# Cross-attention and mixture-of-experts block: the second group's two projections, weight chunk requests and probability copies in new places of a hand-written order

## The chip, the cores and the metric

The kernel runs on one core of one Trainium2 chip. A core has TensorE (PE) for matmuls, VectorE (DVE), ScalarE (ACT), GpSimd (POOL) and SyncE (SP); here SP issues almost all DMAs. The engines run side by side, each through its own queue in order, and wait for each other by semaphores. The metric is the device time of one execution in microseconds (us).

## The reference

One transformer block on x of shape 32 x 100 x 512 with a context of which, by the causal mask, only the first 100 positions count. The first part is cross-attention with 16 heads of 32, the second a feed-forward part: a shared one for every token, and 16 experts that each pick their 12 best tokens per batch element.

```python
# cut to what matters
def attn(Q, K, V, WQ, WK, WV, Wfc, bfc):
    q, k, v = (heads(a @ W.T) for a, W in ((Q, WQ), (K, WK), (V, WV)))
    scores = jnp.einsum('bhqd,bhkd->bhqk', q, k) / jnp.sqrt(32.0)
    p = jax.nn.softmax(jnp.where(causal, scores, -jnp.inf), axis=-1)
    return merge(jnp.einsum('bhqk,bhkd->bhqd', p, v)) @ Wfc.T + bfc

def ffn(h, gate_w, Wg, Wu, Wd, Ws_g, Ws_u, Ws_d):
    w, idx = jax.lax.top_k(softmax(h @ gate_w.T).transpose(0, 2, 1), cap)
    out = scatter_add(idx, (gelu(h[idx] @ Wg.T) * (h[idx] @ Wu.T)) @ Wd.T * w)
    return out + (gelu(h @ Ws_g.T) * (h @ Ws_u.T)) @ Ws_d.T

x = x + attn(layernorm(x), ctx, ctx, ...)
x = x + ffn(layernorm(x), ...)
```

## The kernel before

Everything is float32 in and out. Each large matmul is done in three terms: an operand is split into a high part (rounded to the matmul's type, by a ScalarE copy) and a low part (the difference, by VectorE or POOL), and high x high, high x low and low x high are summed in PSUM (`mm3`, whose matmuls all carry line 56). So every operand of such a matmul costs a copy on one engine and a subtraction on another before TensorE can use it.

**Attention.** The 3200 tokens are cut into 8 blocks of 400 (4 batch elements), and the heads into 4 groups of 4. One *unit* u is one head group of one block, so there are 32 units (NU = 32). Per unit: project q (`qproj`), compute the scores of 4 x 4 pairs (`scores`, tile sc, line 240), take the row maxima on VectorE (`sm_max`, line 251), subtract them on POOL (`sm_sub`, line 260), exponentiate on ScalarE (`sm_exp`, line 264), sum on VectorE (`sm_sum`, line 269), multiply by the reciprocal on POOL (`sm_mul`, line 275), transpose the probabilities on TensorE (`p_turn`, line 281, called through `turns`), copy them from PSUM on ScalarE (`p_keep`, line 286, called through `keeps`), multiply with v (`values`, line 296), split the result and store it to DRAM (`y_keep`, lines 101, 102, 306). The softmax works in two halves (index 0 and 1) of 800 columns. The loop is pipelined by hand: while unit u is projected, u-1 is in its softmax and u-2 in its values.

**Feed-forward.** The tokens are cut into 9 groups of 3, 2, 3, 3, 3, 3, 3, 3 and 2 tiles of 128. For each group an object `Prep` makes the input: load y (`load_y`, tiles yh and yl) and x (`load_x`), add the bias on POOL (`bias`, line 1023), project y with Wfc (`fc`: 12 matmuls of 512 columns in a PSUM tile), add (`add`, line 1032), layer norm (`stats`, `rsqrt`, `norm`, lines 1038 to 1053), store for the experts' gathers, transpose (`turn`, line 963 on TensorE), and router logits (`logits`, `tokens`). Then `job` runs 8 steps f over chunks of the shared weights: 24 gate and up matmuls (tile gu), then 9 (6 for a group of two tiles) down matmuls (tile dn) of the step before. A weight chunk is 768 KB: `chunk_load` asks for the next one in turn, at most two are held raw, and the request for another waits until one of them has been split (`chunk_cast` and `chunk_low` by thirds, or `chunk_split` whole).

**The hand-over** is `last_units`, in which the last units' steps and the first groups' preparation are written out one after the other. The engines PE, ACT, DVE and SP run in the order in which their instructions are written there (`manual_schedule`); POOL too inside attention. Group 0 is projected during the last three units. Of group 1 (two tiles), the first tile is projected at the end of `last_units`, and the second in step f = 2 of group 0's job, from the tables that `run` fills; `early` counts what is already done. Only two PSUM tiles named kv and two named ms serve all projections and transposes there: a tile is free again only once its reader is done.

Of the kernel before, what the change touches and what calls it, by code (L numbers as in the profile page):

```python
# [60 lines left out]
def attention(tc, K, F):  # L61
    nc = tc.nc
    with ExitStack() as ctx, ExitStack() as kvctx:
# [143 lines left out]
        def kload(u):  # L207
            sb, c = divmod(u, NC4)
            kt = ktp.tile([128, SB], F32, name="kt")
            nc.sync.dma_start(kt, K.kD[:, c, sb * SB:(sb + 1) * SB])  # L210
            cur["k", u] = kt
# [50 lines left out]
        def sm_exp(u, hb):  # L262
            pv = cur["p", u, hb][1]
            nc.scalar.activation(pv, pv, AF.Exp)  # L264
# [24 lines left out]
        def values(u):  # L289
            sb, c = divmod(u, NC4)  # L290
            ys = ps_ms.tile([128, NC4, 128], F32, name="ms")
            for b in range(4):
                pt, v = cur["pt", u, b], cur["v", sb, b]
                for h in range(4):
                    d0 = c * 128 + 32 * h
                    nc.tensor.matmul(ys[32 * h:32 * h + 32, b, 0:S], v[:, d0:d0 + 32],  # L296
                                     pt[:, h, :], start=True, stop=True)
            cur["y", u] = ys
# [86 lines left out]
        def turns(u, *bs):  # L385
            for b in bs:
                p_turn(u, b)

        def keeps(u, *bs):
            for b in bs:  # L390
                p_keep(u, b)
# [8 lines left out]
        def last_units(pr):  # L400

            gp, mt = nc.gpsimd, pr.pt

            def maxes(u):
                for hb in range(2):
                    sm_max(u, hb)
                    sm_sub(u, hb)

            u = NU - 3
            scores(u - 1)  # L410
            kload(u)
            for i in range(pr.nt):
                pr.load_x(i)
            y_keep(u - 3)
            kload(u + 1)
            vload(nsb - 1)
            F.chunk_load()
            maxes(u - 1)
            qkeep(u, qproj(u))
            turns(u - 2, 0, 1)  # L420
            keeps(u - 2, 0, 1)
            turns(u - 2, 2, 3)
            sm_exp(u - 1, 0)
            keeps(u - 2, 2, 3)
            sm_exp(u - 1, 1)
            for hb in range(2):
                sm_sum(u - 1, hb)
                sm_mul(u - 1, hb)
            pr.fc(0)
            values(u - 2)  # L430

            u = NU - 2
            scores(u - 1)
            pr.add(0)
            y_keep(u - 3)
            F.chunk_load()
            pr.bias(0)
            maxes(u - 1)
            pr.bias(1)
            pr.stats(0)  # L440
            pr.rsqrt(0)
            qkeep(u, qproj(u))
            turns(u - 2, 0, 1)
            sm_exp(u - 1, 0)
            keeps(u - 2, 0, 1)
            sm_exp(u - 1, 1)
            pr.fc(1)
            for hb in range(2):
                sm_sum(u - 1, hb)
                sm_mul(u - 1, hb)  # L450
            turns(u - 2, 2, 3)
            keeps(u - 2, 2, 3)
            F.chunk_cast(0, 0)
            pr.norm(0)
            pr.add(1)
            kload(u + 1)
            values(u - 2)

            u = NU - 1
            scores(u - 1)  # L460
            y_keep(u - 3)
            pr.store(0)
            pr.bias(2)
            pr.stats(1)
            pr.rsqrt(1)
            maxes(u - 1)
            pr.norm(1)
            qkeep(u, qproj(u))
            F.ask(1, lambda: ps_kv.tile([128, D], F32, name="kv"))
            F.preps[1].load_x(0)  # L470
            F.preps[1].load_x(1)
            turns(u - 2, 0, 1)
            sm_exp(u - 1, 0)
            keeps(u - 2, 0, 1)
            sm_exp(u - 1, 1)
            pr.fc(2)
            sm_sum(u - 1, 0)
            sm_mul(u - 1, 0)
            pr.store(1)
            turns(u - 2, 2, 3)  # L480
            keeps(u - 2, 2, 3)
            sm_sum(u - 1, 1)
            sm_mul(u - 1, 1)
            pr.pt = lambda: ps_kv.tile([128, D], F32, name="kv").rearrange("p (c t) -> p c t", c=NC4)
            pr.turn(0)
            pr.pt = mt
            values(u - 2)
            pr.add(2)
            pr.turn(1)
            pr.stats(2)  # L490
            F.chunk_cast(0, 1)
            pr.rsqrt(2)

            scores(u)
            y_keep(u - 2)
            F.chunk_low(0, 0, gp)
            F.chunk_low(0, 1, gp)
            maxes(u)
            turns(u - 1, 0, 1)
            keeps(u - 1, 0, 1)  # L500
            turns(u - 1, 2, 3)
            keeps(u - 1, 2, 3)
            values(u - 1)
            pr.norm(2)
            sm_exp(u, 0)
            sm_sum(u, 0)
            sm_mul(u, 0)
            pr.turn(2)
            F.preps[1].fc(0)
            sm_exp(u, 1)  # L510
            sm_sum(u, 1)
            sm_mul(u, 1)
            y_keep(u - 1)
            pr.store(2)
            F.chunk_cast(0, 2)
            scctx.close()
            F.open_gu()
            F.begin(pr.done())
            F.chunk_low(0, 2, gp)
            F.preps[1].bias(0)  # L520
            F.preps[1].add(0)
            for i in range(3):
                F.chunk_cast(1, i)
                F.chunk_low(1, i, gp)
            F.preps[1].bias(1)
            turns(u, 0, 1)
            keeps(u, 0, 1)
            pr.logits()
            turns(u, 2, 3)
            keeps(u, 2, 3)  # L530
            F.begun()
            values(u)
            pr.tokens()
            y_keep(u)
# [91 lines left out]
class FeedForward:  # L626
# [186 lines left out]
    def run(self):  # L813
# [3 lines left out]
        def at(d, f, *calls):  # L817
            d.setdefault(f, []).extend(calls)
# [5 lines left out]
        for g in range(ng):  # L824
            mid, post = {}, {}
            p = preps.get(g + 1)
            early = 1 if g == 0 else 0
            if early:
                p.pm, p.pt = self.prep(1).pm, self.prep(1).pt
            if g == 0:  # L830
# [2 lines left out]
            if g < ng - 1:  # L833
                own = g == ng - 3
                z = 2 if own else 0
                if not early:
                    at(post, 0, *[lambda p=p, i=i: p.load_x(i) for i in range(p.nt)])
                if own:
                    for i in range(q.nt):
                        at(mid, i, lambda i=i: q.fc(i))  # L840
                        at(post, i, lambda i=i: q.ln(i))
                        at(post, 1 + i, lambda i=i: q.store(i))
                        at(mid, 2 + i, lambda i=i: q.turn(i))
                    at(post, 3, q.keep)
                    at(mid, 4, q.logits)
                    at(post, 4, q.tokens)
                    at(post, 1, lambda p=p: p.load_y())
                at(post, 1, *[lambda p=p, i=i: p.bias(i) for i in range(2 * early, p.nt)])
                for i in range(p.nt):
                    f = z + 1 + i  # L850
                    if i >= early:
                        at(mid, f, lambda p=p, i=i: p.fc(i))
                    if own:
                        at(post, f, lambda p=p, i=i: p.ln(i))
                        at(post, min(f + 1, 7), lambda p=p, i=i: p.store(i))
                        at(mid, min(f + 2, 7), lambda p=p, i=i: p.turn(i))
                    else:
                        f = (2, 3, 3)[i]
                        at(post, f, lambda p=p, i=i: p.ln(i))
                        at(post, f + 1, lambda p=p, i=i: p.store(i))  # L860
                        if g == ng - 2:
                            at(mid, 4 + i, lambda p=p, i=i: p.turn(i))
                        else:
                            at(post, f + 2, lambda p=p, i=i: p.quarters(i))
                            at(post, f + 3, lambda p=p, i=i: p.turn(i))
                if g == ng - 2:
                    at(mid, 7, p.logits)
                    at(post, 7, p.tokens)
                elif not own:
                    at(post, 7, p.logits)  # L870
                if g == ng - 4:
                    at(post, 6, q.load_y)
                    at(post, 6, q.load_rows)
                    at(post, 7, q.bias)
                    preps[ng - 2] = self.prep(ng - 2)
                elif g + 2 < ng:
                    at(post, 7, lambda g=g: self.ask(g + 2))
# [450 lines left out]
```

## Time and profile before

| | us |
|---|---|
| median of three runs | 1685.66 (1684.33 to 1686.12) |
| profiled execution | 1681.56 |
| its span, first to last instruction | 1679.3 |
| TensorE busy in the span | 1658.3 |
| start, 0 to 41 us of the span: TensorE busy | 34.38 of 41.00 |
| attention, 41 to 322: TensorE busy | 278.59 of 281.00 |
| hand-over, 322 to 374: TensorE busy | 45.70 of 52.00 |
| feed-forward, 374 to the end: TensorE busy | 1299.60 of 1305.30 |

In the views that follow, a line of the order of time has the start in us, the duration, the engine, the line of the kernel, the operation, output <- inputs by the program's tile names, the shape and the number of instructions; a bracket holds the idle time before it and what ended that. A line of the waits has who waited for whom, the total in us, how often, and the longest. Matmul durations overlap one another, so that the start of the next instruction tells more than the end of one.

### The profile page before, as it was taken

To read this page: it belongs to the slowest core of one execution; us is meant where nothing else is said; L and a number is where in the kernel's file an instruction comes from. 1 tells how busy PE (TensorE), PEld (TensorE's weight loads), DVE (VectorE), ACT (ScalarE), POOL (GpSimd) and SP (SyncE) were. 2 spreads that over 40 slices of the span, in tenths; PEclk is the share of its full clock that TensorE was granted. 3 is DMA by queue.
4 is the path that set the end of the run, shared out by engine and by line. 5 is a ranking of instruction groups with operands and counts; after the bars stand their busy time and mean duration, and the time that the engine had idled before them with its cause. 6 is when DMAs were issued, how large, how long until landed. Compare 5 with 4: busy or idle time off the path is not lost.

```text
span 1679.3 us, 28090 instructions
## 1 busy us (share of the span) xinstructions
PE 1658.3 (99%) x10879; PEld 1523.6 (91%) x10879; DVE 919.0 (55%) x2199; ACT 679.5 (40%) x1088; POOL 625.2 (37%) x542
## 2 busy tenths in 40 slices
PE   8999999989999999999999999999999999999999
PEld 7988888879889898989899999999999999999998
DVE  4878777665433434343555555555555555555542
ACT  4555555553111111112334444444444444444442
POOL 3778777670110011010243344333344333344011
PEclk9999999999999999999999999999999999999999
DMA  7555544555312223211455555455555455555452
GB/s 214 158 169 184 156 157 147 179 196 178 109 62 88 76 83 131 82 44 42 144 166 151 165 169 144 158 163 148 162 167 151 154 161 155 159 161 159 136 164 63
DMA packets 107125, 237.47 MB, mean 141 GB/s; under 512 B 14161, under 2 KB 58418, under 8 KB 106992
## 3 DMA queue, kind: packets, MB, share of 16 engines
q1 hardware_dynamic: 93632, 209.99, 38.4%
q0 software_dynamic: 12944, 25.22, 7.9%
q8 instruction: 85, 1.39, 0.4%
q10 hardware_dynamic: 416, 0.48, 0.1%
q14 instruction: 48, 0.39, 0.1%
HBM read 181.90 MB, written 53.73 MB: 140 GB/s over the span
## 4 chain that ended last, share of the span: by engine, by line
PE 93%; DMA 2%; DVE 1%; ACT 1%; POOL 1%; issue 1%; SPq 0%; ACTq 0%; POOLq 0%; DVEq 0%
PE gu L56 49%; PE dn L56 24%; PE kv L56 11%; PE m L56 3%; PE ms L281 2%; PE ms L296 1%; PE sc L240 1%; POOL p L260 1%; DMA v<-vD 1%; DVE p L251 1%; ACT pt L286 1%; PE ms L171 0%; DMA kD<-kk 0%; DMA x<-x 0%; DMA yh<-yD 0%
## 5 line engine op out<-in xcount | busy, mean ns | idle before, releaser
L56 PE MATMUL gu<-xh,whl 128*128 128x384 f32 (+1 forms) x3200 | 642.4, 332 | 0.0
L56 PEld LDWEIGHTS gu<-xh,whl 128*128 128x128 f32 x3200 | 556.7, 188 | 19.9 <-issue 1.7
L56 PE MATMUL dn<-whl,hh 128*128 128x512 f32 x1168 | 366.1, 394 | 0.0
L738 DVE TENSOR_TENSOR whl<-wraw,whl 128x1536 fp32r<-128x1536 f32 x142 | 249.8, 1759 | 203.2 <-ACT whl L737 181.6
L943 POOL DMA_INDIRECT gx<-xnD,iq x180 | 226.8, 1260 | 359.3 <-DVE big L974 299.8
L56 PE MATMUL gu<-xl,whl 128*128 128x384 f32 (+1 forms) x1600 | 336.7, 332 | 0.0
L56 PEld LDWEIGHTS gu<-xl,whl 128*128 128x128 f32 x1600 | 279.9, 188 | 0.0
L772 ACT CAST hh<-g 128x384 fp32r<-128x384 f32 (+1 forms) x200 | 100.9, 505 | 408.3 <-DVE g L769 384.2
L769 DVE TENSOR_TENSOR g<-g,gu 128x384 f32<-128x384 f32 (+1 forms) x200 | 108.4, 542 | 257.5 <-PE gu L56 252.9
L56 PEld LDWEIGHTS dn<-whl,hh 128*128 128x128 f32 x1168 | 215.5, 188 | 36.2 <-ACT hh L772 0.4
L737 ACT CAST whl<-wraw 128x1536 fp32r<-128x1536 f32 x142 | 210.0, 1479 | 61.8 <-PE dn L56 58.7
L56 PE MATMUL dn<-whl,hl 128*128 128x512 f32 x584 | 230.6, 395 | 0.0
L768 ACT ACTIVATE g<-gu 128x384 f32<-128x384 f32 (+1 forms) x200 | 96.3, 481 | 241.4 <-PE gu L56 240.7
L773 DVE TENSOR_TENSOR hl<-g,hh 128x384 fp32r<-128x384 f32 (+1 forms) x200 | 111.2, 556 | 114.2 <-ACT hh L772 113.7
L986 POOL DMA_INDIRECT out_dram<-x,isl x48 | 77.8, 1620 | 171.7 <-ACT x L985 161.9
L56 PEld LDWEIGHTS dn<-whl,hl 128*128 128x128 f32 x584 | 109.7, 188 | 25.3 <-DVE hl L773 0.2
L260 POOL TENSOR_TENSOR p<-p,mx 100x800 f32<-100x800 f32 x64 | 96.7, 1532 | 64.2 <-DVE mx L251 61.1
L275 POOL TENSOR_TENSOR p<-p,sm 100x800 f32<-100x800 f32 x64 | 101.2, 1582 | 4.7 <-DVE sm L270 3.9
L251 DVE CUSTOM_DVE_ANT_0 p<-sc,mask 100x100 f32<-100x100 f32 x512 | 95.4, 256 | 0.0
L1023 POOL TENSOR_TENSOR x<-x,bfc 128x512 f32<-128x512 f32 x23 | 30.6, 1347 | 155.1 <-DMA x<-x 119.5
L975 ACT CAST xh<-big 128x512 fp32r<-128x512 f32 x59 | 36.6, 621 | 101.2 <-DVE big L974 101.2
L269 DVE TENSOR_REDUCE sm<-p 100x8 f32<-100x800 f32 x64 | 63.1, 986 | 23.7 <-ACT p L264 23.7
(160 smaller groups left out, 1638.1 us busy)
## 6 DMA issues: line engine op xcount, KB each, us to landing
wraw<-wE SPq DMA_DIRECT2D x144, 768.0 KB
yD<-y SPq DMA_DIRECT2D x31, 400.0 KB
xt<-x SPq DMA_DIRECT2D x32, 200.0 KB
vD<-vt SPq DMA_DIRECT2D x25, 256.0 KB
kt<-kD SPq DMA_DIRECT2D x32, 200.0 KB
v<-vD SPq DMA_DIRECT2D x8, 800.0 KB
xnD<-xn SPq DMA_DIRECT2D x25, 256.0 KB
out_dram<-x SPq DMA_DIRECT2D x25, 256.0 KB
```

The costliest lines, as they stand in the source:

```text
L56: r = nc.tensor.matmul(out, t[0][a], t[1][b], start=(first and i == 0), stop=(last and i == n - 1))
L251: nc.vector.tensor_tensor_reduce(out=p[:, bb, h, :], in0=sc[:, h, cs], in1=mask, scale=ISCALE, scalar=NEG, op0=ALU.add, op1=ALU.max, accum ...
L260: nc.gpsimd.tensor_tensor(pv, pv, mx[:, :, None].to_broadcast([S, 8, S]), ALU.subtract)
L275: nc.gpsimd.tensor_tensor(pv, pv, sm[:, :, None].to_broadcast([S, 8, S]), ALU.mult)
L737: nc.scalar.copy(h, r)
L738: nc.vector.tensor_tensor(l, r, f32(h), ALU.subtract)
L768: nc.scalar.activation(g[:, 0:t], pg[:, 0:t], AF.Gelu)
L769: nc.vector.tensor_tensor(g[:, 0:t], g[:, 0:t], pu[:, 0:t], ALU.mult)
L772: nc.scalar.copy(hh[:, 0:t], g[:, 0:t])
L773: nc.vector.tensor_tensor(hl[:, 0:t], g[:, 0:t], f32(hh[:, 0:t]), ALU.subtract)
L943: nc.gpsimd.indirect_dma_start(out=g[:, k, :], out_offset=None, in_=self.K.xn.rearrange("t (a f) -> (t a) f", f=128), in_offset=bass.Indir ...
L986: ins = nc.gpsimd.indirect_dma_start(out=self.K.out, out_offset=bass.IndirectOffsetOnAxis(ap=r.isl[:, i:i + 1], axis=0), in_=o, in_offset= ...
```

## The change

Four things move; apart from that the instructions are the same.

- The first two requests for weight chunks (`chunk_load`) are written later: the first after group 0's first projection in the step u = NU-3, the second after the kt load at the end of the step u = NU-2.
- The casts of chunk 0 move back: the first from the step u = NU-2 to just ahead of the last scores, the second from there to between the two exponentials of the last unit. The low part of its second third moves from ahead of the last unit's maxima to after its second exponential.
- In the step u = NU-1 the first two probability copies are written ahead of the first exponential.
- Group 1's two projections stand inside the last unit: the first right after the last scores, the second after the transposes of unit 30. The values of unit 30 follow after the third tile's transpose. The second projection is no longer in step f = 2 of group 0's job, and both adds and both biases of group 1 are in `last_units`; bias comes after the split of chunk 1.

```diff
@@ step u = NU - 3
             vload(nsb - 1)
-            F.chunk_load()
             maxes(u - 1)
...
             pr.fc(0)
+            F.chunk_load()
             values(u - 2)
@@ step u = NU - 2
             y_keep(u - 3)
-            F.chunk_load()
             pr.bias(0)
...
-            F.chunk_cast(0, 0)
             pr.norm(0)
             pr.add(1)
             kload(u + 1)
+            F.chunk_load()
             values(u - 2)
@@ step u = NU - 1
             turns(u - 2, 0, 1)
+            keeps(u - 2, 0, 1)
             sm_exp(u - 1, 0)
-            keeps(u - 2, 0, 1)
             sm_exp(u - 1, 1)
...
             pr.stats(2)
-            F.chunk_cast(0, 1)
+            F.chunk_cast(0, 0)
             pr.rsqrt(2)
 
             scores(u)
             y_keep(u - 2)
             F.chunk_low(0, 0, gp)
-            F.chunk_low(0, 1, gp)
+            F.preps[1].fc(0)
             maxes(u)
             turns(u - 1, 0, 1)
             keeps(u - 1, 0, 1)
             turns(u - 1, 2, 3)
             keeps(u - 1, 2, 3)
-            values(u - 1)
+            F.preps[1].fc(1)
             pr.norm(2)
             sm_exp(u, 0)
+            F.chunk_cast(0, 1)
             sm_sum(u, 0)
             sm_mul(u, 0)
+            sm_exp(u, 1)
+            F.chunk_low(0, 1, gp)
             pr.turn(2)
-            F.preps[1].fc(0)
-            sm_exp(u, 1)
+            values(u - 1)
             sm_sum(u, 1)
             sm_mul(u, 1)
...
             F.chunk_low(0, 2, gp)
-            F.preps[1].bias(0)
             F.preps[1].add(0)
+            F.preps[1].add(1)
             for i in range(3):
                 F.chunk_cast(1, i)
                 F.chunk_low(1, i, gp)
+            F.preps[1].bias(0)
             F.preps[1].bias(1)
@@ FeedForward.run
-            early = 1 if g == 0 else 0
+            early = 2 if g == 0 else 0
...
-                at(post, 1, *[lambda p=p, i=i: p.bias(i) for i in range(2 * early, p.nt)])
+                at(post, 1, *[lambda p=p, i=i: p.bias(i) for i in range(early, p.nt)])
```

## The prediction

> **What bounds the kernel now.** I read the page first, then TensorE's own waits after the stage that the change edits, then the order of time of TensorE's instructions inside that stage, then those of the engines that release them.
>
> ```profile
> span 1679.3 us, 28090 instructions
> PE 1658.3 (99%) x10879; PEld 1523.6 (91%) x10879; DVE 919.0 (55%) x2199; ACT 679.5 (40%) x1088; POOL 625.2 (37%) x542
> ```
>
> TensorE is busy for 99% of the span. From 374 us on, where the feed-forward part runs alone, its waits come to two lines:
>
> ```profile
> PE m L963 <- DVE xl L965: 1.5, 1, 1.5
> PE m L1196 <- DVE x L1032: 0.2, 1, 0.2
> ```
>
> So a microsecond saved or lost before 374 should arrive at the end unchanged. Only two things can move the time: TensorE's work, which this change leaves equal in number, and TensorE's gaps in the hand-over between attention and feed-forward. These are the gaps (brackets: idle time, and what ended it):
>
> ```profile
> 348.33 1.09 PE L56 MATMUL kv<-wfh,yl 128*128 128x512 f32 x4
> 350.23 0.86 PE L281 MATMUL ms<-ident,p 100*100 100x100 f32 x8 [0.81 <-ACT pt L286]
> 350.93 0.67 PE L963 MATMUL kv<-ident,xn 128*128 128x128 f32 x4
> 351.80 0.89 PE L296 MATMUL ms<-pt,v 100*32 100x100 f32 x32 [0.20 <-ACT pt L286]
> 352.63 0.75 PE L963 MATMUL ms<-ident,xn 128*128 128x128 f32 x4
> 353.31 0.96 PE L240 MATMUL sc<-kt,q 32*100 32x100 f32 x32
> 354.87 0.52 PE L281 MATMUL ms<-ident,p 100*100 100x100 f32 x4 [0.60 <-DVE xl L965]
> 356.07 0.89 PE L281 MATMUL ms<-ident,p 100*100 100x100 f32 x8 [0.68 <-DVE y L102]
> 357.26 0.55 PE L281 MATMUL ms<-ident,p 100*100 100x100 f32 x4 [0.29 <-ACT pt L286]
> 357.74 1.09 PE L296 MATMUL ms<-pt,v 100*32 100x100 f32 x32
> 360.89 0.72 PE L963 MATMUL ms<-ident,xn 128*128 128x128 f32 x4 [2.06 <-DVE xn L1053]
> 361.37 1.17 PE L56 MATMUL kv<-wfh,yh 128*128 128x512 f32 x4
> ...
> 364.24 0.87 PE L56 MATMUL gu<-xh,whl 128*128 128x384 f32 x4
> ...
> 383.79 1.08 PE L56 MATMUL m<-wfh,yh 128*128 128x512 f32 x4
> ```
>
> The gaps sum to 0.81+0.20+0.60+0.68+0.29+2.06 = 4.64 us: the most that this change can win. Two instructions of other engines explain the largest:
>
> ```profile
> 358.84 1.91 DVE L1053 TENSOR_SCALAR xn<-x,mv,rs 128x512 f32<-128x512 f32 x1
> ...
> 358.93 3.20 POOL L260 TENSOR_TENSOR p<-p,mx 100x800 f32<-100x800 f32 x2
> ```
>
> The transpose at 360.89 needs the normalised third tile, which VectorE writes only after the 16 maxima of the last unit (356.01 to 358.9). Meanwhile TensorE has nothing else in its order.
>
> **The change part by part.**
>
> *Weight chunks asked for later.* I compared the orders on SP's queue. No SP instruction stands between the old and the new place of the first request, so it keeps its place behind the load of v. The second only changes places with one kt load (old issues: 335.31 and 335.87). kt is needed by the scores at 353.31 and the second chunk by casts behind 363; both DMAs had landed by 347 in the trace's landing records. Cost 0. The cover is at least 6 us for each.
>
> *First cast (chunk_cast(0,0)) taken out of the unit before.* ScalarE stood 1.23 us at 343.27 waiting for the chunk, and VectorE's y low part (L102, 344.31) then waited 0.27 us for ScalarE's y, queued behind that cast. Without it ScalarE's y starts at 342.7, when the values end; VectorE goes on at once, and the maxima, the first subtraction on POOL (347.28, which waited 0.35 us for them) and the second (ends 350.47) come 0.3 us earlier.
>
> *Probability copies ahead of exponentials (unit 31's step).* The first two copies run at 346.4 instead of 349.6, so the transposes of 350.23 start at 349.42: the 0.81 us gap closes. But copies 3 and 4 stand behind both exponentials, and the second exponential waits for POOL: 350.16, 0.87 us long, so copy 3 starts near 350.95 instead of 351.28. The values need copy 3's buffer and start 0.52 us after it begins (351.28 to 351.80), now at 351.47. The gap moves to the values; what remains is a gain of 0.33 us, all of it from the previous paragraph. The last scores start at 352.98.
>
> *Both projections (Prep.fc, 12 matmuls each) between softmax steps.* One costs 361.37 to 364.24 = 2.87 us of TensorE. New order with durations from the rows above (next start minus start):
> - scores 0.90, to 353.88;
> - fc(0) 2.87, to 356.75. It covers both the 0.60 and the 0.68 gap, whose releasers (VectorE at 354.7 and 356.0, now 0.3 earlier) are done by then;
> - four transposes of p: the first copy starts 0.61 us after the first transpose (354.87 to 355.48), and its buffer lets the third go 0.55 us later (the last copy of the pair to the next transpose, 356.71 to 357.26). So 0.61+0.55+0.35+0.39 = 1.90 us against 1.38 without waits, to 358.65;
> - fc(1) 2.87, to 361.52. It covers the 2.06 gap: maxima end at 358.6, norm between 359.1 and 360.8;
> - third tile's transpose 0.48, values 0.83, to 362.83.
>
> The gate matmuls also need ScalarE's xh (0.76 after the transpose starts, as 360.89 to 361.65, then 0.64) and, a quartet (0.70) later, VectorE's xl (0.61 after xh starts, then 0.84 as 354.03 to 354.87): 361.52+0.76+0.61+0.84 = 363.73, less 0.70 is 363.03. This ends last, by 0.2 us. The gate thus starts at an effective 363.03 instead of 364.24: 1.21 us.
>
> *The projection that leaves the feed-forward part* (383.79 to the next down matmul at 386.57): 2.78 us, off TensorE's path at a place without gaps.
>
> Sum: 1.21 + 2.78 = **3.99 us, taken as 4.0** (the 0.33 is inside the 1.21).
>
> *What each moved step meets.* fc(0) now needs yh and yl at 353.88 and 355.74 (two thirds through). Their issues (348.52, 349.45 on SP) wait only for the third projection, which does not move; by the landing records yh is complete at 352.35 and yl at 354.06. Slack 1.5 and 1.7 us. Were they later, all of TensorE's queue would stand behind fc(0): transposes, copies, values. POOL: one of the two low parts (1.28 us each) leaves the front of the last subtractions, which then start at 357.45 instead of 358.93, when the first maxima are done; the other goes between the multiplications, ends near 364.4, and is needed a quartet before the gate's end, about 366.5. The second multiplication ends near 366 and is needed by transposes near 369. The low parts of chunk 1 end at 371.0 (was 372.2). Bias after add: same instructions, ending at 373.5, needed at 387. VectorE's second add moves from 397 to 365, where it had 3.75 us of idle time. Chunk 4 lands 0.65 us before ScalarE turns to it, and its request moves with that chain; its matmuls come 5 us later. All 0.
>
> [...] VectorE's norm took 1.91 us at 358.84 and 1.81 at 341.63, both beside POOL's tensor work, but 0.58 at 348.51. [...]
>
> **The rivals.**
> - *Hand-offs eat part of it.* The transpose-copy-transpose ladder, or xh and xl ahead of the gate, cost 0.7 to 1.3 us more, or the 0.33 does not come. For it: the margin there is 0.2 us. Against: all links are measured ones. Gain 2.7 to 3.3 us: about 1682.7.
> - *All gaps close.* Gain 4.64 plus the 0.58 gap at 341 us: 1680.4. Against it: the ladder and the values' wait remain by my own working.
> - *The projection waits for its input (the slower side).* fc(0) stands first in TensorE's queue with yl still coming. Each microsecond beyond 355.74 delays everything: the gain is gone when yl lands at 359.7, 5.7 us later than now; 9.1 us late gives 1689. For it: this group's input loads were never waited for, so nothing has tested them. Against: before these two loads the DMA rate was near 0 (348 to 349.5 us), so there is nothing to queue behind, and the change adds no bytes there.
> - *The change doesn't do what it says:* true of the requests (above), not of the projections.
>
> **How the numbers follow.** The profiled execution took 1681.56 us (span 1679.3 and 2.3 around it); 4.0 less is 1677.6. The three runs shown have a median of 1685.66, 4.1 above the profiled one; the saving is in absolute time, so the forecast is 1681.7. The runs differ by 1.8 us; with 0.2% (3.4 us) as what can be told from no change, 4.0 is just outside. Chances: forecast 0.57, hand-offs 0.23, all gaps 0.05, slower 0.15 (late inputs and what I have not seen). The forecast's own range is 1680.6 to 1682.6, and some of it counts as no change; the hand-offs nearly all do. Faster 0.57, same 0.28, slower 0.15. Range: 1679.6 (all gaps, with 0.8 us of run-to-run difference) to 1687.0 (a little of the slower case).
>
> **What would show it.** In the changed profile: the 2.06 us gap before the third tile's transpose gone, the gate's first matmul near 363.0, no projection (m<-wfh,yh) in the third feed-forward step, that step's end 4 us earlier, TensorE's waits after 374 unchanged. The prediction is wrong if a kv<-wfh,yh projection carries a DMA wait, if the gate starts after 364, or if a weight wait turns up between 375 and 410.

## The result and the profile after

| | before | after |
|---|---|---|
| median, 11 runs each | 1684.31 us (1681.89 to 1686.12) | 1681.38 us (1677.50 to 1682.06) |
| profiled execution | 1681.56 us | 1681.51 us |
| its span | 1679.3 us | 1679.6 us |

The ratio is 0.9973, with a 95% interval of 0.9965 to 0.9981: a gain of 4.5 us (3.2 to 5.9); the medians differ by 2.9 us. The forecast was 1681.7 us, with a gain of 3.99 us worked out. The medians, the range and the sign agree with it. Yet the two *profiled* executions take the same time, and in the changed one the gate starts at 367.29 (1.40 us of that is a later start of the hand-over), which by the prediction's own signs (near 363.0; wrong if after 364) speaks against it. A gain that the medians show and the profiles don't has to be explained, and most of the experiments of the next section do that.

First, TensorE's waits of the changed kernel from 374 us to the end (who waited for whom, total us, times, longest):

```profile
PE m L965 <- DVE xl L967: 1.5, 1, 1.5
PE ms L296 <- ACT pt L286: 0.3, 1, 0.3
PE m L1198 <- DVE x L1034: 0.2, 1, 0.2
```

The feed-forward part waits as before: the 0.3 us are the last values (374.79), which stand at the border of this window. Next, the order of time of TensorE's instructions in the hand-over of the changed kernel:

```profile
350.74 0.85 PE L281 MATMUL ms<-ident,p 100*100 100x100 f32 x8
351.43 0.67 PE L965 MATMUL kv<-ident,xn 128*128 128x128 f32 x4
354.40 1.45 PE L296 MATMUL ms<-pt,v 100*32 100x100 f32 x32 [2.30 <-ACT pt L286]
355.78 1.13 PE L965 MATMUL ms<-ident,xn 128*128 128x128 f32 x4
356.84 1.48 PE L240 MATMUL sc<-kt,q 32*100 32x100 f32 x32
358.25 1.19 PE L56 MATMUL kv<-wfh,yh 128*128 128x512 f32 x4
...
361.13 0.85 PE L281 MATMUL ms<-ident,p 100*100 100x100 f32 x8
362.37 0.86 PE L281 MATMUL ms<-ident,p 100*100 100x100 f32 x8 [0.39 <-ACT pt L286]
363.01 1.17 PE L56 MATMUL kv<-wfh,yh 128*128 128x512 f32 x4
...
365.90 0.63 PE L965 MATMUL ms<-ident,xn 128*128 128x128 f32 x4
366.46 0.90 PE L296 MATMUL ms<-pt,v 100*32 100x100 f32 x32
367.29 0.96 PE L56 MATMUL gu<-xh,whl 128*128 128x384 f32 x4
...
386.23 0.86 PE L56 MATMUL gu<-xh,whl 128*128 128x384 f32 x4
386.92 0.62 PE L56 MATMUL dn<-whl,hh 128*128 128x512 f32 x2
```

From 358.25 on it is the picture that was forecast: neither projection waits for anything, the ladder of transposes has the one wait of 0.39 us, the third tile's transpose (365.90) has none where 2.06 us stood, and gate and up of the third step are followed at once by down (386.92), with no projection between. Ahead of it two things were not forecast: a wait of 2.30 us before the values (forecast: 0.72), and behind it values, transposes and scores that take 1.45, 1.13 and 1.48 us, against 0.89, 0.75 and 0.96 before.

What the values wait for, followed back through the order of time of the other engines of the changed kernel:

```profile
343.20 3.20 DVE L1055 TENSOR_SCALAR xn<-x,mv,rs 128x512 f32<-128x512 f32 x1
...
346.93 0.56 DVE L102 TENSOR_TENSOR y<-ms,y 128x400 fp32r<-128x400 f32 x1
...
343.12 3.01 POOL L275 TENSOR_TENSOR p<-p,sm 100x800 f32<-100x800 f32 x2
...
349.88 3.19 POOL L260 TENSOR_TENSOR p<-p,mx 100x800 f32<-100x800 f32 x2 [0.61 <-DVE mx L251]
...
351.44 0.87 ACT L264 ACTIVATE p<-p 100x800 f32<-100x800 f32 x1 [2.76 <-POOL p L260]
353.10 0.87 ACT L264 ACTIVATE p<-p 100x800 f32<-100x800 f32 x1 [0.79 <-POOL p L260]
353.87 0.87 ACT L286 COPY pt<-ms 100x400 f32<-100x400 f32 x2
```

The same pair of instructions in the profile before, VectorE's normalisation of the first tile (`norm(0)`) and GpSimd's two multiplications:

```profile
341.63 1.81 DVE L1053 TENSOR_SCALAR xn<-x,mv,rs 128x512 f32<-128x512 f32 x1
...
341.55 3.28 POOL L275 TENSOR_TENSOR p<-p,sm 100x800 f32<-100x800 f32 x2
```

In both profiles the normalisation (line 1055 in the changed kernel) starts 0.08 us behind the first multiplication. In the changed kernel it ends 0.27 us behind the second and takes 3.20 us, and each multiplication takes 1.53 us; before, it took 1.81 us and ended 0.37 us behind the first multiplication, and there the second took 1.80 us, so that the two took 3.28 us instead of 3.01. The starts don't tell which of the two outcomes it will be. Behind the normalisation queue the low part of y, the maxima, through them GpSimd's subtractions, and then the second exponential, behind which copies 3 and 4 stand in ScalarE's order.

The granted clock of TensorE in three consecutive stretches of the changed kernel (columns: stretch, its length, busy time of PE, PEld, DVE, ACT and POOL, granted clock, share and rate of the DMA engines):

```profile
351.16:354.57 3.41, 1.11 (x18) 0.92 (x19) 2.29 (x6) 2.34 (x4) 2.77 (x3) 1.00 0.98 301
354.57:357.98 3.41, 3.41 (x64) 2.79 (x60) 2.32 (x5) 1.69 (x5) 2.18 (x2) 0.50 0.67 230
357.98:361.39 3.41, 3.41 (x31) 2.73 (x24) 3.38 (x25) 0.46 (x2) 2.15 (x4) 1.00 0.29 104
```

For 3.41 us right behind the wait the clock is 0.50, and the three long steps lie in that stretch.

### The profile page after: what moved, and what is told of

Same layout as the page of the kernel before. It is cut to its first block, busy times and chain, and to the rows that moved or that the text cites. A ratio compares the mean times of both kernels' runs of the same rounds, so it can differ in the third digit from the quotient of the medians.

```text
span 1679.6 us, 28091 instructions
## 1 busy us (share of the span) xinstructions
PE 1660.7 (99%) x10879; PEld 1526.4 (91%) x10879; DVE 920.8 (55%) x2199; ACT 679.2 (40%) x1088; POOL 625.2 (37%) x542
## 3 DMA queue, kind: packets, MB, share of 16 engines
q8 instruction: 85, 1.39, 0.3%
## 4 chain that ended last, share of the span: by engine, by line
PE 93%; DVE 2%; ACT 1%; POOL 1%; DMA 1%; issue 1%; SPq 0%; ACTq 0%; POOLq 0%; DVEq 0%
PE gu L56 49%; PE dn L56 24%; PE kv L56 10%; PE m L56 3%; PE ms L281 2%; PE ms L296 2%; POOL p L260 1%; PE sc L240 1%; DVE p L251 1%; DMA kD<-kk 1%; ACT pt L286 1%; PE ms L171 0%; DVE y L102 0%; PE m L1109 0%; DMA raw<-wA 0%
```

## The experiments

In the table, all durations come from each kernel's profiled execution. Waits are those from unit 30's scores on. "Hand-over" runs from the start of unit 30's scores (342.58 in the profile before, 343.98 after) to the first gate matmul; that leaves out what comes earlier, which differs by up to 2.5 us between the profiles (the scores of the first unit alone start between 41.24 and 43.14 us). "Rest" is from there to the end of the span. The forecast's hand-over was 363.03 - 342.58 = 20.45 us. Each ratio is to the runs of the kernel before that were made in the same rounds; their medians lie between 1684.31 and 1684.74 us.

| kernel | median us (runs) | ratio to before (95%) | norm(0) us | waits over 0.7 us | half clock | hand-over | rest |
|---|---|---|---|---|---|---|---|
| before | 1684.31 (11) | 1 | 1.81 | 0.81, 2.06 | no | 21.66 | 1315.06 |
| e0, before again, two profiles | 1685.37, 1686.02 | | 3.21, 3.21 | 1.92, 2.07 in each | twice in each | 25.44, 25.34 | 1314.98, 1315.03 |
| after | 1681.38 (11) | 0.9973 (0.9965-0.9981) | 3.20 | 2.30 | once | 23.31 | 1312.31 |
| e1, after again | 1680.01 (7) | 0.9971 (0.9960-0.9982) | 3.21 | 2.30 | once | 23.42 | 1312.40 |
| e2, projections alone | 1679.01 (6) | 0.9968 (0.9955-0.9980) | 3.21 | 1.94 | no | 21.84 | 1312.20 |
| e3, all but them | 1682.63 (13) | 0.9992 (0.9983-1.0000) | 1.81 | 0.77, 0.83 | once | 21.57 | 1315.26 |
| e4, after, all copies first | 1677.98 (5) | 0.9961 (0.9948-0.9975) | 3.21 | none | no | 20.89 | 1312.36 |
| e5, after, norm(0) on ScalarE, late | 1683.40 (13) | 0.9995 (0.9986-1.0003) | 0.82 | 2.33 | no | 22.25 | 1314.02 |
| e7, e4 and e5 | 1680.84 (11) | 0.9977 (0.9968-0.9986) | 0.81 | 0.71 | no | 21.69 | 1314.10 |
| e8, after, norm(0) on ScalarE, early | 1679.71 (6) | 0.9965 (0.9953-0.9977) | 0.81 | 1.11 | no | 20.48 | 1314.08 |
| e9, before, norm(0) on ScalarE, early | 1686.98 (13) | 1.0012 (1.0004-1.0021) | 0.81 | 1.67, 2.08 | no | 22.46 | 1316.92 |
| e10, e4 and norm(0) as in e8 | 1678.79 (5) | 0.9958 (0.9944-0.9971) | 0.81 | none | no | 19.76 | 1314.13 |
| e11, after, wait filled | 1679.59 (5) | 0.9964 (0.9951-0.9978) | 3.20 | 0.79 | no | 21.71 | 1312.48 |

### Both kernels again, unaltered

> The changed kernel once more, unaltered. Its runs lie in two groups, near 1677.9 and near 1681.6. [...] Theory 2 (start-up): the groups differ in what happens before 45 us of the span, and the hand-over looks alike in both, with the 3.20 us norm and the gap in it.

The changed kernel again: 1680.01 us, ratio 0.9971 (0.9960 to 0.9982). Its profile repeats all of the first: norm(0) 3.21, wait 2.30, half clock (355.81 to 359.22), hand-over 23.42. So the wait is no accident of one execution. Whether a quick run has a norm(0) near 1.8 us and no half clock in the hand-over, or parts from the others by 45 us of the span, could not be put to the test, as the profile did not fall among the quick runs; and four of these seven runs lie between the two groups, which are less sharp than they looked. Taken together, the 18 runs of this kernel have a median of 1680.1.

> The kernel before once more, unaltered, for its trace alone: its median is 2.9 us above the execution that was profiled first. Theory 1 (hand-over): an execution near 1684 shows the norm of the first tile (L1053 near 342) at 3.2 us, or TensorE at half clock for 3.41 us between 350 and 364, or both, and the gate starts 2 to 3.5 us later than 21.66 us after the scores of 342 us. Theory 2 (start-up): all of the difference is there by 45 us of the span.

> As the look before, to see whether the outcome of the norm and of the clock changes from execution to execution of one kernel (then they are chance) or stays (then they belong to the kernel).

The kernel before, twice: 1685.37 and 1686.02 us. Both look different from the profile that the forecast was made on. TensorE's order of time in the first of the two (release in brackets), and the granted clock in the stretches behind those two waits:

```profile
351.54 0.86 PE L281 MATMUL ms<-ident,p 100*100 100x100 f32 x8 [1.92 <-ACT pt L286]
...
363.23 1.05 PE L963 MATMUL ms<-ident,xn 128*128 128x128 f32 x4 [2.07 <-DVE xn L1053]
```

```profile
353.17:356.58 3.41, 3.41 (x56) 2.79 (x60) 2.22 (x5) 1.59 (x4) 2.29 (x2) 0.50 0.69 240
...
363.41:366.82 3.41, 3.41 (x11) 2.83 (x11) 2.93 (x5) 2.80 (x6) 2.58 (x2) 0.50 0.00 0
```

norm(0) took 3.21 us in both, the 0.81 us wait of the first profile is 1.92 here, and behind each of the two waits the clock is halved for 3.41 us. The hand-over takes 25.4 us. The profile before, 4.1 us under the median of the three runs shown with it, was an execution in which norm(0) took 1.81 us and the clock stayed at 1.00 behind every wait of the hand-over. That explains most of the equal profiled times: they compare a lucky execution of one kernel (hand-over 21.66) with an unlucky one of the other (23.31). Taken apart, the changed kernel's span is 1.40 us longer up to unit 30's scores, 1.65 us longer in the hand-over and 2.75 us shorter in the rest, together 0.3 us longer. Unlucky against unlucky the hand-over gains 25.4 - 23.4 = 2.0 us, and the rest 2.7. How often each outcome comes was not counted: all four of these executions lie above the medians of their kernels.

### The two halves of the change

e2 is the kernel before with only the projections, their adds and biases, and the values of unit 30 moved (the second projection is left out of step f = 2 accordingly):

```diff
             F.chunk_low(0, 1, gp)
+            F.preps[1].fc(0)
             maxes(u)
...
-            values(u - 1)
+            F.preps[1].fc(1)
             pr.norm(2)
...
             pr.turn(2)
-            F.preps[1].fc(0)
+            values(u - 1)
...
             F.preps[1].add(0)
+            F.preps[1].add(1)
...
```

> The kernel before with the two projections of group 1 moved (and add and bias after them) and nothing else: chunk requests, casts and copies as before. If the gain is the projections' (my sum: 3.99 less the 0.3 that the cast and copies bring), the median is 3.5 to 4 us under before, within 1 us of the changed kernel. If the gain came from casts, copies or requests, it is within 1.5 us of before.

1679.01 us, ratio 0.9968: 5.4 us under the kernel before, more than the 3.5 to 4 expected. TensorE's order of time in e2:

```profile
351.20 0.86 PE L281 MATMUL ms<-ident,p 100*100 100x100 f32 x8 [1.94 <-ACT pt L286]
...
362.82 0.63 PE L965 MATMUL ms<-ident,xn 128*128 128x128 f32 x4
```

The 2.06 us wait is gone and with it, in this execution, any half clock, though norm(0) took 3.21 us here too and the wait ahead of the transposes stood at 1.94 us. Its hand-over of 21.84 us less the 1.19 us by which its values came later than in the profile before (10.41 against 9.22 us from the start of the scores) is 20.65: by this estimate, which takes the later start of the values as passed on in full, the projections alone gained 21.66 - 20.65 = 1.0 us there, and another 1315.06 - 1312.20 = 2.86 us in the rest.

e3 is the reverse, the changed kernel with the projections back in their old places (bias stays where the change put it):

```diff
             F.chunk_low(0, 0, gp)
-            F.preps[1].fc(0)
             maxes(u)
...
-            F.preps[1].fc(1)
+            values(u - 1)
             pr.norm(2)
...
             pr.turn(2)
-            values(u - 1)
+            F.preps[1].fc(0)
...
```

> The changed kernel with the projections put back where they were before (one after the third tile's transpose, one in step f = 2); requests, casts and copies as in the change. By my sum 0.3 us under before, not to be told from it: ratio 0.999 to 1.001. If requests, casts and copies carry the gain, ratio near 0.997.

1682.63 us, ratio 0.9992 (0.9983 to 1.0000): no change that can be told. So the whole of the gain that can be told from no change belongs to the projections, as the sum said. In e3's profile norm(0) took 1.81 us, as in the profile before, and so the copies' order can be read without that disturbance: the values start 8.81 us after the scores instead of 9.22, 0.41 us earlier (forecast 0.33), with 0.77 us of the wait left (forecast 0.72).

### Where the copies stand

e4 takes the changed kernel and puts copies 3 and 4 ahead of the second exponential as well:

```diff
             sm_exp(u - 1, 0)
-            sm_exp(u - 1, 1)
             pr.fc(2)
...
             turns(u - 2, 2, 3)
             keeps(u - 2, 2, 3)
+            sm_exp(u - 1, 1)
```

> The changed kernel with copies 3 and 4 of that step also written ahead of the second exponential. Theory 1: the values no longer wait for the exponential that POOL holds up, so the 2.30 us gap (and the half clock after it) goes and the group near 1681.6 moves down by 2 us or more; in the fast group the remaining 0.7 us gap goes as well: median 1677 to 1678.5, one group rather than two. Theory 2: two groups 3.6 us apart remain, and the median goes down by 0.7 at most.

1677.98 us, all five runs between 1677.38 and 1678.69: 2 us under the changed kernel's median in e1, and the ratio to the one before is 0.9961 (6.6 us; the intervals of the two ratios overlap). TensorE's order of time in e4:

```profile
351.62 0.89 PE L296 MATMUL ms<-pt,v 100*32 100x100 f32 x32 [0.64 <-ACT pt L286]
...
354.72 1.19 PE L56 MATMUL kv<-wfh,yh 128*128 128x512 f32 x4 [0.63 <-DVE xl L967]
```

norm(0) still took 3.21 us, yet the values wait 0.64 us instead of 2.30: once the copies no longer stand behind an exponential, its lateness reaches only work that isn't needed yet. The hand-over falls by 2.4 us (23.31 to 20.89); a wait of 0.63 us for a transposed tile's low part is new.

### Is norm(0) the cause?

e5 moves norm(0), and no other tile's, from VectorE to ScalarE, which computes rs * x + nm with nm = -mean * rs made on GpSimd:

```diff
-        nc.vector.tensor_scalar(xn, self.xb[i], mv[:, 0:1], rs, ALU.subtract, ALU.mult)
+        if (self.t0, i) == (0, 0):
+            nm = F.stp.tile([128, 1], F32, name="nm")
+            nc.gpsimd.tensor_scalar(nm, mv[:, 0:1], rs, -1.0, ALU.mult, ALU.mult)
+            nc.scalar.activation(xn, self.xb[i], AF.Identity, bias=nm, scale=rs)
+        else:
+            nc.vector.tensor_scalar(xn, self.xb[i], mv[:, 0:1], rs, ALU.subtract, ALU.mult)
```

> The changed kernel with the norm of group 0's first tile on ScalarE (with its bias made by one small POOL operation), so that VectorE no longer waits for POOL's multiplications there. Theory 1: maxima, subtractions and exponentials come 1.2 to 1.6 us earlier, the 2.30 us gap shrinks to 0.7, the half clock behind it goes: one group, 1677 to 1678. Theory 2: still two groups, near 1678 and 1681.5.

> Copies 3 and 4 ahead of the second exponential and the norm of the first tile on ScalarE together. If each removes its own wait, 0.5 to 1.5 us under the kernel with the copies alone (1677.98), that is 1676.5 to 1677.5; if the second one only removes what the first already covers, no difference from it.

1683.40 us, and 1680.84 with e4's copies: 2.0 to 3.4 and 2.9 us slower than without the edit, which none of the expectations had. The edit was badly placed. Orders of time of ScalarE and of GpSimd in e5:

```profile
345.60 0.82 ACT L1058 ACTIVATE xn<-x,nm,rs 128x512 f32<-128x512 f32 x1 [2.92 <-POOL nm L1057]
...
345.30 0.27 POOL L1057 TENSOR_SCALAR nm<-mv,rs 128x1 f32<-128x1 f32 x1
```

nm stood in GpSimd's queue behind both multiplications, so ScalarE waited 2.92 us, and its y, on which VectorE's chain hangs, stood behind it. So the values still waited 2.33 us, now for another reason. This profiled execution (1681.52 us) is 1.9 us under e5's median; what the slower ones contain was not seen. These two decide nothing on norm(0), but e5 tells something of the clock, below.

e8 makes nm right behind rs, ahead of the multiplications:

```diff
         nc.gpsimd.tensor_tensor(rs, rs, F.K.nhalf[:, 0:1], ALU.pow)
+        if (self.t0, i) == (0, 0):
+            nm = F.stp.tile([128, 1], F32, name="nm")
+            nc.gpsimd.tensor_scalar(nm, mv[:, 0:1], rs, -1.0, ALU.mult, ALU.mult)
...
```

> The changed kernel with the first tile's normalisation on ScalarE instead of VectorE, its bias (minus mean times rs) made on GpSimd right behind rs, so ahead of the two multiplications by 1/sum; in e5 the bias stood behind them and so ScalarE waited 2.92 us. Theory 1 (VectorE's 3.2 us normalisation at 342 to 343, held up by GpSimd's two multiplications of 100x800, delays maxima, subtractions and exponentials, and so the last copies): the wait of the values before the last scores falls from 2.30 to about 0.8 us, no half-clock stretch stands behind it, and the time is 1677.5 to 1679.0 in all runs, near e4. Rival (the normalisation is late for another reason, or something else sets the exponentials): the wait stays over 1.8 us and the time stays at 1680 to 1681.5.

ScalarE, VectorE and TensorE in e8, by their orders of time:

```profile
344.31 0.81 ACT L1060 ACTIVATE xn<-x,nm,rs 128x512 f32<-128x512 f32 x1
...
345.53 0.58 DVE L102 TENSOR_TENSOR y<-ms,y 128x400 fp32r<-128x400 f32 x1 [0.93 <-ACT y L101]
...
353.94 0.89 PE L296 MATMUL ms<-pt,v 100*32 100x100 f32 x32 [1.11 <-ACT pt L286]
...
365.32 0.97 PE L56 MATMUL gu<-xh,whl 128*128 128x384 f32 x4
```

VectorE's y starts 0.69 us after the scores, against 2.95 in the changed kernel; the wait of the values falls from 2.30 to 1.11 us, no clock is halved, and the hand-over takes 20.48 us, where 20.45 had been forecast. So norm(0) is the cause of 1.19 us of the wait of 2.30 us in the profile of the changed kernel; without these no clock was halved behind the wait. The time misses both expectations (1677.5 to 1679.0, or 1680 to 1681.5): the median, 1679.71 us, is lower by only 0.3 to 1.7 us than the two medians of the changed kernel, and the runs still spread from 1678.16 to 1681.21; the rest, from the gate on, is 1.77 us longer (last section), which hides part of the gain. The profiled execution is the slowest of the six; its scores start late, at 344.84.

> The kernel before with the same edit of the first tile's normalisation. Theory 1: the wait of the probability turns for GpSimd falls from 1.92 to 0.8 us or less, the wait of 2.06 us behind the last scores stays with its half-clock stretch; 1682.0 to 1683.5 us, ratio 0.9985 to 0.9995. Rival (before doesn't suffer from that normalisation): 1684.0 to 1685.0 and a ratio of 1.

The same edit in the kernel before gave 1686.98 us, slower by 0.12% (0.04 to 0.21%), where a gain or no change was expected. ScalarE's order of time in e9:

```profile
343.74 0.62 ACT L721 CAST whl<-wraw 128x512 fp32r<-128x512 f32 x1 [1.31 <-DMA wraw<-wE]
344.27 0.81 ACT L1058 ACTIVATE xn<-x,nm,rs 128x512 f32<-128x512 f32 x1
```

There the first cast of the weight chunk stands ahead of the normalisation, and waits 1.31 us for its DMA. VectorE's y comes 2.57 us after the scores, hardly better than 2.95. That is one part of why nothing was gained; the longer rest, here 1.9 us, is another. This profiled execution (1684.17 us) is 2.8 us under e9's median and shows no half clock; what the slower runs contain was not seen.

> The best version so far (e4, all four copies ahead of the second exponential) with the same edit. Theory 1: the copies no longer wait for the exponential, so the earlier exponentials can only help the turns of the last unit: 1677.3 to 1678.2, the same as e4 within 0.5 us. Rival (ScalarE's added 0.6 us stands in the way of its copies): 1678.5 or more.

1678.79 us, ratio 0.9958, not to be told from e4 (0.9961); the median lies in the range of the rival, but not for its reason. Its hand-over is the shortest of all, 19.76 us; the rest, 1.77 us longer than e4's, takes that back. The simple e4 is the better version.

### Is it the wait that halves the clock?

e11 leaves the wait of the values as it is and puts TensorE work nobody needs into it: the four transposes of the first tile are issued four times, into the same places.

```diff
-        for b in range(NC4):
+        for b in list(range(NC4)) * (4 if fill else 1):
             nc.tensor.transpose(tv[:, b, :], rv[:, b], self.K.ident)
...
```

> The changed kernel with the four transposes of the first normalised tile issued four times over, the same results into the same places: about 1.9 us of TensorE work that nobody needs, in the wait of 2.30 us ahead of the values. Nothing of that wait is taken away. Theory of the clock (the gap itself halves the clock for 3.41 us and so costs about 1.4 us more than its length): the half-clock stretch behind the values is gone, values 0.89, transposes 0.75 and scores 0.96 us again instead of 1.45, 1.13 and 1.48, and the median is 0.8 to 1.5 us below that of the changed kernel, at 1678.9 to 1680. Rival (the half clock falls there by chance of its own and gaps of this length don't matter): the median stays at 1680 to 1681.4, or rises by up to 1 us where the wait was short.

TensorE's order of time in e11:

```profile
350.50 2.11 PE L965 MATMUL kv<-ident,xn 128*128 128x128 f32 x16
353.40 0.89 PE L296 MATMUL ms<-pt,v 100*32 100x100 f32 x32 [0.79 <-ACT pt L286]
354.23 0.75 PE L965 MATMUL ms<-ident,xn 128*128 128x128 f32 x4
354.91 0.96 PE L240 MATMUL sc<-kt,q 32*100 32x100 f32 x32
...
364.82 0.97 PE L56 MATMUL gu<-xh,whl 128*128 128x384 f32 x4
```

norm(0) took 3.20 us and the values started 10.29 us after the scores (10.42 in the changed kernel): nothing was won there. But the clock stays at 1.00, the three steps have their old lengths, and the hand-over falls from 23.31 to 21.71 us. Less the 0.13 us at the values, 1.47 us of that is the clock. The median is 1679.59 us, 1.8 us under the first eleven runs of the changed kernel and 0.4 under the seven of e1, so the profile shows this effect and the medians don't settle it. With twelve useless matmuls none of the five runs took longer than 1680.14.

Not every wait of this length does it. The granted clock and TensorE's busy time in e5, whose values waited 2.33 us:

```profile
349.96:353.37 3.41, 2.02 (x16) 1.64 (x14) 2.72 (x17) 1.24 (x2) 3.01 (x2) 1.00 0.68 207
353.37:356.79 3.42, 2.48 (x69) 2.11 (x69) 2.83 (x6) 2.64 (x6) 3.04 (x2) 1.00 1.02 340
```

In the first profile of each kernel, the ends of the half-clock stretches lie on one grid of 3.413 us (in the changed kernel 26.89 and 357.99, 97 periods apart; in the kernel before one stretch, from 14.78 to 21.61, two periods long). In the hand-over, such stretches begin at 354.57 in the changed kernel, at 355.81 in e1, at 360.17 in e3, and in the first profile of e0 at 353.17 and 363.41, three periods apart; so the grid stands elsewhere relative to the work in each. A period of it is called a cell here. Where a hand-over has no half clock, the place of its cells is the author's estimate, carried on in steps of 3.413 us from the half-clock stretches at the start of the profile (in the kernel before, 94 steps from 21.61 to 342.45). By it the wait of e5 falls across two cells, with 1.39 and 0.93 us idle in them. Over the fourteen profiles, counting TensorE's idle time per cell of the hand-over: each of the six cells with 1.62 to 2.30 us idle was followed by a half-clock cell. Of those with 1.54 us or less one was, in e3, with 1.12 us idle. That one remains unexplained; the cells with 1.27 to 1.54 us of idle time in before, e2, e3, e5 and e9 were not followed by one. But idle time alone does not decide it. Here are two cells with the same idle time, 1.62 us, each with the one that follows, first in e1's hand-over and then in the attention part of the kernel before:

```profile
352.40:355.81 3.41, 1.79 (x48) 1.52 (x52) 2.87 (x6) 2.31 (x5) 2.63 (x3) 1.00 1.02 344
355.81:359.22 3.41, 3.41 (x38) 2.75 (x30) 3.30 (x16) 1.32 (x3) 2.00 (x4) 0.50 0.22 82
...
164.97:168.38 3.41, 1.79 (x12) 1.48 (x11) 3.05 (x23) 1.49 (x3) 3.05 (x3) 1.00 0.64 195
168.38:171.79 3.41, 3.41 (x21) 2.82 (x20) 2.20 (x5) 2.49 (x6) 3.31 (x4) 1.00 0.30 69
```

In the first the clock was halved, in the second it wasn't. The first holds 48 matmuls, most of them small ones, the second 12, most of them large; whether that is the reason was not tested. In e11 the wait, unfilled, would have lain wholly in one cell by the same estimate (350.39 to 353.80), as in the changed kernel (351.16 to 354.57), so that the filling and not the grid would have kept the clock up there. What has to come together besides a wait stays open.

## Why the prediction was right, step by step

*Requests for chunks: 0.* Held. No wait for weights appears in TensorE's waits behind 374.

*First cast taken out of the unit before: 0.3 us.* Right in direction, under-valued. ScalarE's y starts 0.13 us after the scores, against 1.22 before. Where norm(0) takes 1.81 us (e3) this reaches the maxima with 0.41 us; e9 shows the cast's place in the queue costing 1.31 us of ScalarE's time when something is put behind it.

*Copies ahead of exponentials: the 0.81 us wait moves to the values, 0.72 remains.* This is the step that failed. The move to the values is right, and in e3 it is 0.77. But the working carried over the 1.81 us of norm(0), from the one profile there was, as given, and so forecast the values 0.33 us earlier than before; they came 1.20 us later (10.42 us from the scores against 9.22). norm(0) took 3.2 us in seven of the nine profiles that have it on VectorE, and in those of the changed kernel the wait was 2.30 us instead of 0.72. The prediction set GpSimd's work beside the durations of norm(2) and norm(0) (1.91 and 1.81 us), but worked out anew only the time of norm(2), where it turned out harmless (0.69 us, at 362.37), and passed over norm(0), which sits beside two GpSimd multiplications. The 3.20 us of norm(0) end 0.27 us behind the second multiplication, and where it took 1.81 us the two multiplications took 0.27 us longer. That norm(0) stood back for both multiplications in the one case, and the second of them for norm(0) in the other, is the author's reading of these times; no trace shows such a wait. What decides between the two outcomes no run shows.

*fc(0) and fc(1) as cover: 1.21 us of the hand-over.* Held. e8, without the norm(0) disturbance, takes 20.48 us where 20.45 was forecast, in part by luck: its values start 0.21 us later than forecast and the gate follows them 0.18 us sooner. e2's projections gain 1.0 of 1.21. The ladder of transposes has 363.01 - 361.13 = 1.88 us (forecast 1.90), the gap of 2.06 us is gone in every kernel with moved projections, no projection waited for yh or yl. The gate itself started at 367.29, not 363.0, for reasons outside this step: unit 30's scores came 1.40 us later in this execution (343.98; the first unit's were 1.64 us later already), and the hand-over took 23.31 us instead of 20.45. Of the 2.83 us above e8's 20.48, norm(0) accounts for 1.23 (e11 against e8), the half clock for 1.47 and an earlier start of the values in e11 for 0.13 (e11 against the changed kernel). These are differences between single executions.

*The projection out of step 2: 2.78 us.* Held: the rest behind the gate falls from 1315.06 to 1312.31, 2.75 us.

*The clock.* The sum held it constant, and that is its second gap. In both later profiles of the kernel before a half clock stands behind each of two waits, of 1.92 and 2.07 us, and this change takes away the second wait. So against these two it gains more (2.0 + 2.7 us), against the lucky execution profiled first, from the scores on, less (2.75 - 1.65 = 1.1 us). The errors came out small in the total by luck: 3.99 us forecast, 4.5 (3.2 to 5.9) measured. Nor was the sum of the gaps, 4.64 us, the most that could be won: e4 is 6.6 us under the kernel before.

*The basis.* The forecast subtracted the gain from the median of three runs, not from the profiled execution that it was derived from, and so came near 1681.4. That too holds some luck: over eleven runs the median before is 1684.31, 1.35 us lower, and the medians differ by 2.9 us only. Subtracting from the profiled time would have given 1677.6, which is where the five quickest of the eleven runs of the changed kernel lie (1677.5 to 1678.3; the other six: 1681.4 to 1682.1). Whether those five are executions in which norm(0) takes 1.8 us was not seen in a trace, since both profiles of this kernel fell among the slower ones. The clock has a part in it: each run has its mean granted clock on record, and a stretch of 3.41 us at half clock lowers it by 0.001 (3.41 x 0.5 / 1680). Of the 18 runs, the four with 0.999 took 1677.3 to 1679.0 us, the two with 0.996 took 1681.7 and 1682.1. Whether these stretches lie in the hand-over or at the start of the program, the mean doesn't tell.

*The rivals.* "Hand-offs eat part of it" came closest to what the profile shows, by another hand-off than those named. "All gaps close" needs e4's order of copies. "The projection waits for its input" never happened.

## What to carry to other kernels

One profile is one draw: where two engines work side by side and an instruction's duration changes from execution to execution (norm(0) in the kernel before: 1.81 us in one profile, 3.21 in two), look at several executions of the kernel before, and ask which duration is the usual one before a sum is made with it. A copy that frees a buffer for TensorE belongs ahead of an exponential that waits for other engines; all of such copies, not the first half (e4: 1677.98 us against 1680.0 in the same rounds). Taking away a long wait on TensorE can be worth more than its length: in the changed kernel the clock was 0.50 for 3.41 us behind a wait of 2.30 us, and in e11 even useless work in the wait shortened the hand-over by 1.6 us.

## What the runs showed of the hardware

- A VectorE normalisation of 128x512 in float32 took 0.58 us at its shortest (the second tile's, at 351.10 in the changed kernel), and beside two GpSimd multiplications of 100x800 either 1.81 us, with the multiplications 0.27 us longer, or 3.2 us. The kernel before showed either (1.81 us in the first profile, 3.21 in both of e0).
- Waits of TensorE of 1.92 to 2.30 us were in six cases followed by 3.41 us at half clock, on a grid of 3.413 us; others (2.06 in before, 1.94 in e2, 2.33 in e5, 2.08 in e9) were not; there, with the cells placed by estimate, none had more than 1.54 us idle. In the changed kernel the half clock cost 1.47 us, measured against e11.
- Kernels with the normalisation on ScalarE ran slower *behind* the gate by 1.7 to 1.9 us, though no wait there differs. The same stretch of the feed-forward part, in the changed kernel and in e10 (columns as above; x is the number of matmuls that fit):

```profile
900.00:1500.00 600.00, 600.00 (x3159) 562.33 (x3158) 333.37 (x359) 271.68 (x359) 239.77 (x180) 1.00 0.54 158
```

```profile
900.00:1500.00 600.00, 600.00 (x3151) 561.20 (x3150) 331.97 (x358) 271.99 (x359) 240.50 (x180) 1.00 0.54 157
```

Eight matmuls fewer in 600 us are 0.25%, or 1.5 us, at full clock and without a wait. All five kernels with that edit show it (3150 to 3152), none of the nine profiles of the others does (3157 to 3160). More than half of it sits in the down matmuls: in this stretch, from the first of two on hh to the one on hl behind them the mean time from start to start is 465.6 ns in e10 (285 times) against 461.7 in e4 (287 times), and from the one on hl to the next on hh 233.7 against 233.1; from a quartet of gate and up matmuls to the next it differs by 3.5 ns at most. More instructions alone don't do it: e11 has twelve and doesn't show it. The five alone have one more small tile, nm; whether that matters was not tested. It is enough to hide the gain of a microsecond elsewhere.
